# A decoder layer on one NeuronCore: layernorm's last step moved to VectorE, scratch parts written once per batch, and cross-attention divided by its sums in PSUM

## The chip, the core and the metric

The kernel runs on one core of a Trainium2 chip. A core has a matrix engine (TensorE, "PE" in the profile; its weight loads are "PEld"), three engines for elementwise work (VectorE, "DVE"; ScalarE, "ACT"; GpSimd, "POOL"), and SyncE ("SP"), which here only issues DMAs. Matrix products land in PSUM (8 banks of 128 partitions x 512 float32 here); everything else works in SBUF. The metric is the device time of one execution in microseconds, lower is better; the time of a kernel is the median of its runs.

## The reference

32 batches of 128 tokens with 128 features go through a post-norm decoder layer. Cut to what matters:

```python
x = layernorm(x + self_attention(x))          # 16 heads of 8; q = k = x, values x, then @ weight
x = layernorm(x + cross_attention(x, ctx))    # 16 heads of 8, scores masked to |i - j| <= 64
x = layernorm(x + two_layers(x))              # each: local attention (8 heads of 64), gated feed-forward

def layernorm(x):
    return (x - mean(x)) / sqrt(var(x) + 1e-5)

# cross-attention, per batch and head
scores = Q @ K.T / sqrt(8), masked
out    = softmax(scores) @ V                  # = (exp(scores - max) @ V) / sum(exp(scores - max))
y      = concat(out) @ Wo.T + bo
```

Each of the two layers has one more layernorm (with gain and bias) ahead of its feed-forward. So a batch meets five layernorms: after self-attention, after cross-attention, one in each layer, one at the end; 160 in all.

## The kernel before, in words

The 32 batches are cut into 10 groups of 1 to 4 (`SIZES`). Each group passes four stages: self-attention, cross-attention, layer 0, layer 1. A stage is a Python generator that records operations (`op(engine, ns, function, reads, writes, ...)`, L84) and yields after each batch; a due time `STARTS[g] / G + k * LAG * CLOSE[g]` with a spread per batch (end of the kernel) sorts the pieces of all stages into one list, so that several groups in different stages are interleaved.

`Plan.issue` (L132) then makes the real order by hand of a planner: every operation has a declared cost in ns, every buffer belongs to a ring (`Ring`, `Val`) of a few tiles, and the planner takes, engine by engine, the operation that can start first by these costs, looking at most `AHEAD` operations past the first one not yet placed and preferring the older one among those within `NEAR` ns. An operation that needs a buffer waits until the ring has one; `hold` reserves a buffer early; `KEEP` sets how many of a ring are left for older values; `port=True` keeps GpSimd and VectorE operations on SBUF from overlapping in the plan. The result is a fixed instruction order per engine; semaphores between engines do the rest. Rings: `m` (the 8 PSUM banks), `big` (23 wide tiles), `mid` (17), `xb` (6), `xc` (4), `sm` (24 small ones), `slots` (12 scratch areas in HBM).

What the change and the prediction touch:

- `layernorm` (L377): statistics on VectorE (L382, L389), the reciprocal root and the bias by four small GpSimd instructions (L397 to L400), and the last step x * r + q, one ScalarE instruction of 128x128 per batch (L407).
- `in_slots` (L494): queries and keys are split into three bfloat16 parts (ScalarE L500, L506; GpSimd L502, L508). Nine DMAs per group and tile write the three parts into nine slots of a scratch area in HBM, each DMA one part into one slot for all batches of the group (L518). `stacked` (L525) reads one batch back with the nine slots on 72 partitions (L528); it waits for all nine writes. Scores (`scores_of`, L540) are products over those 72 rows.
- `cross_batch` (L701): per half of the heads: scores with a mask, row maxima on VectorE (L421), exponentials on ScalarE (L466), transposes (L481) and copies (L488), then the product with the values (L722), whose output holds 32 rows of values and 32 rows of sums, in two column halves of the PSUM tile: `o.t[64 * c : 64 * c + 64, 0:P]`. ScalarE copies this to SBUF (L731). After both halves two transposes (L738) turn it, and VectorE takes a reciprocal of 16 sums per token (L748) and multiplies (L749).
- `cross_attention` (L634): after the batches of a group, `turned` (L362) transposes the result again (L373, one transpose per batch) and copies it (ScalarE, L367), for the projection (L687).
- ScalarE's copies of local attention's products are at L799 and L855, its exponentials at L466; VectorE's work of local attention is at L808, L831, L835, L838, L883 and L884, its residual add at L917; GpSimd's at L811, L812 and L822. Self-attention's products are at L577 and L606, its reciprocals and multiplies at L615 and L616; the projections of the layers at L794, L910, L942 and L962.

Of the kernel before, what the change touches and what calls it, by code (L numbers as in the profile page):

```python
# [11 lines left out]
AF = mybir.ActivationFunctionType  # L12
ALU = mybir.AluOpType
# [14 lines left out]

AHEAD = 290
LAG = 1.35  # L30
RINGS = (23, 17, 6, 4)
KEEP = (2, 4, 6)
NEAR = 60
EARLY = (0.1, 0.2)
CLOSE = (0.9, 0.85, 0.9, 1, 1, 1, 1.15, 1.0, 0.85, 0.95)
SPREAD = (1.3, 1.0, 0.7, 1.5)
LH, LD = 8, 64
# [194 lines left out]
def decoder_kernel(ctx: ExitStack, tc: tile.TileContext, a: dict, out: bass.AP):  # L232
    nc = tc.nc
# [5 lines left out]
    def ring(name, n, keep, shape, dtype=F32, pool=const):  # L239
        return Ring([pool.tile(shape, dtype, name=f"{name}{i}") for i in range(n)], keep)  # L240
# [7 lines left out]
    small = ring("sm", 24, 4, [P, 32])  # L248
# [3 lines left out]
    w_self, w_cross = Val(nothing), Val(nothing)  # L252
    w_layer = [Val(nothing) for _ in range(DEPTH)]
    mtring = ring("mt", 4, 1, [P, P], BF16)

# [3 lines left out]
    def group(v):  # L259
        return v[:, 0:512].rearrange("p (g d) -> p g d", g=G)  # L260
# [116 lines left out]
    def layernorm(src, dst, n):  # L377
# [26 lines left out]
        def apply():  # L404
            x, y = group(src.t), group(dst.t)
            for j in range(n):
                nc.scalar.activation(  # L407
                    y[:, j, :], x[:, j, :], AF.Identity,
                    scale=mv.t[:, 8 + j : 9 + j], bias=mv.t[:, 12 + j : 13 + j],
                )  # L410

        op("ACT", 425 * n, apply, [mv] + ([src] if src is not dst else []), [dst])

# [80 lines left out]
    def in_slots(src, n, keep_src, moving):  # L494
# [17 lines left out]
        for m in moving:  # L512
            t = Val(slots)
            for a in range(3):
                for b in range(3):
                    k = 3 * b + a if m else 3 * a + b
                    op("SP", P * 256 * n / 150,
                       lambda t=t, a=a, k=k: nc.sync.dma_start(  # L518
                           t.t[0:n, k].rearrange("j f t -> f j t"),
                           pv.t[:, a, every].rearrange("p (j t) -> p j t", j=n)),  # L520
                       [(pv, a)], [(t, k)])
            out.append(t)
        return out

    def stacked(t, j):  # L525
        v = Val(big, lambda t: t.bitcast(BF16)[0:72, 0:2048])
        op("SP", 72 * 4096 / 250,
           lambda: nc.sync.dma_start(  # L528
               v.t, t.t[j].rearrange("s (d h) t -> (s d) (h t)", d=8)), [t], [v])
        return v  # L530
# [103 lines left out]
    def cross_attention(g):  # L634
# [24 lines left out]
        def values():  # L659
# [14 lines left out]
           [w_cross], [x1], port=True)  # L674
        on = Val(mid)
        yield
        qs, = in_slots(qT, n, False, (False,))
        ks, = in_slots(kT, n, False, (True,))
        for j in range(n):
            cross_batch(j, stacked(qs, j), stacked(ks, j), vT, on)  # L680
            yield
        onT = turned(on, n)
        yp = Val(mring)

        def project():
            for j in range(n):
                nc.tensor.matmul(  # L687
                    yp.t[:, 128 * j : 128 * j + 128], group(onT.t)[:, j, :], woT,
                    start=True, stop=True,
                )  # L690

        op("PE", n * 228, project, [onT, w_cross], [yp])
        op("DVE", 160 + 135 * n,
# [6 lines left out]

    def cross_batch(j, qs, ks, vT, on):  # L701
        vb = Val(vbring)
# [4 lines left out]
           [vT], [vb])  # L707
        oS = Val(mid)
        for hh in range(2):
# [6 lines left out]

            o = Val(mring)

            def pe(o=o, et=et, hh=hh, vb=vb):
                for b in range(4):  # L720
# [7 lines left out]

            op("PE", 875, pe, [et, vb], [o], hold=[oS], tiling=("columns", "columns"))
            op("ACT", 260,  # L730
               lambda o=o, hh=hh: nc.scalar.copy(  # L731
                   oS.t[:, 128 * hh : 128 * hh + 128], o.t[:, 0:P]),
               [o], [(oS, hh)])
        ot = Val(mring)

        def back(ot=ot, oS=oS):
            for r in range(2):
                nc.tensor.transpose(  # L738
                    ot.t[:, 128 * r : 128 * r + 128], oS.t[:, 128 * r : 128 * r + 128], ident
                )  # L740

        op("PE", 260, back, [oS], [ot])
        rl = Val(small)

        def normal(ot=ot, rl=rl, j=j):
            v = ot.t[:, 0:256].rearrange("p (c s b d) -> p c s b d", c=4, s=2, d=8)
            r = rl.t[:, 0:16].rearrange("p (c b) -> p c b", b=4)
            nc.vector.reciprocal(r, v[:, :, 1, :, 0])  # L748
            nc.vector.tensor_tensor(  # L749
                group(on.t)[:, j, :].rearrange("p (c b d) -> p c b d", b=4, d=8),  # L750
                v[:, :, 0], r.unsqueeze(3).to_broadcast([P, 4, 4, 8]), ALU.mult,
            )

        op("DVE", 560, normal, [ot], [rl, (on, j)])


# [364 lines left out]
```

## Time and profile before

| | us |
|---|---|
| time, median of 3 runs (lowest to highest) | 1290.97 (1290.47 to 1292.42) |
| the profiled execution's own time | 1291.86 |
| its span from first to last instruction | 1290.10 |
| TensorE busy / VectorE busy | 1213.7 / 1003.5 |
| ScalarE busy / GpSimd busy | 1018.7 / 827.3 |
| DMA: bytes moved, mean rate | 91.43 MB, 71 GB/s |

The profile records one execution. Its parts: busy time of each engine; the span in 40 slices of 32 us, one digit per slice (9 is 90% or more); the chain of work that ended last, followed back from the last instruction, with its shares by engine; and groups of instructions, one line each: source line, engine, operation, output and input tiles, shapes and count, then busy time in us, the mean duration in ns, and the idle time of the engine just before these instructions with what ended it. Busy times of overlapping matmuls are not counted twice, so a group's busy time can be less than count times mean. DMAs show in the queue of the engine that issued them (SPq).

### The profile page before, as it was taken

The page shows a single profiled execution, that of the slowest core. Times are in us where ns is not written, and L with a number is a line of the kernel's source. Part 1 is how long each engine was busy: PE and PEld are TensorE (multiplying, and loading weights), DVE is VectorE, ACT ScalarE, POOL GpSimd, SP SyncE. Part 2 cuts the span into 40 slices and gives each one's busy share as a digit, 9 for nine tenths or more (in the row PEclk, how much of TensorE's full clock was granted, in tenths as well). Part 3 has the DMA queues.
Part 4 walks back from the last instruction along what each step waited for, and adds up shares of the span by engine and source line. Part 5 has one row for each costly group of instructions (what it writes and reads, how often), then busy time and mean ns, then how long its engine had stood idle before and what let it go on. Part 6 is the DMA issues. An engine that isn't in the chain of part 4 may idle for free.

```text
span 1290.1 us, 27567 instructions
## 1 busy us (share of the span) xinstructions
PE 1213.7 (94%) x9687; PEld 887.6 (69%) x9730; DVE 1003.5 (78%) x1974; ACT 1018.7 (79%) x2920; POOL 827.3 (64%) x1094
## 2 busy tenths in 40 slices
PE   7899999999999999989999999999999999999886
PEld 3777767767676776767677787667666776567654
DVE  2678788768986888777787887777899877888774
ACT  4467677878797779867888888778898897999874
POOL 1775676755867675854687476654876647975353
PEclk9899999999999999999999999999999999999988
DMA  8768443242415150434105141422300010000000
GB/s 219 215 158 226 119 101 82 54 121 52 95 32 148 29 119 7 92 83 120 51 2 131 30 120 32 99 60 61 84 3 10 4 35 1 9 2 1 2 9 17
DMA packets 173546, 91.43 MB, mean 71 GB/s; under 512 B 155488, under 2 KB 161504, under 8 KB 173152
## 3 DMA queue, kind: packets, MB, share of 16 engines
q1 hardware_dynamic: 173408, 89.67, 27.7%
q8 instruction: 77, 1.26, 0.4%
q14 instruction: 61, 0.50, 0.1%
HBM read 49.79 MB, written 39.85 MB: 69 GB/s over the span
## 4 chain that ended last, share of the span: by engine, by line
PE 60%; POOL 12%; ACT 11%; DVE 10%; issue 3%; DMA 2%; SPq 1%; POOLq 0%; ACTq 0%; DVEq 0%
PE m L794 8%; PE m L481 7%; PE m L606 6%; PE m L577 5%; PE m L942 5%; ACT big L466 4%; PE m L869 4%; PE m L910 4%; POOL sm L811 4%; PE m L898 3%; PE m L849 3%; PE m L540 3%; PE m L962 3%; PE m L722 3%; POOL big L626 3%
## 5 line engine op out<-in xcount | busy, mean ns | idle before, releaser
L466 ACT ACTIVATE big<-m,sm 128x128 f32<-128x128 f32 x1024 | 322.6, 399 | 49.9 <-DVE sm L421 41.8
L421 DVE TENSOR_REDUCE sm<-m 128x4 f32<-128x512 f32 x384 | 244.8, 680 | 79.0 <-PE m L540 38.6
L626 POOL TENSOR_TENSOR big<-big 128x512 f32<-128x512 f32 (+2 forms) x192 | 164.1, 854 | 90.0 <-DVE big L616 36.0
L811 POOL TENSOR_TENSOR sm<-sm,nhalf 128x16 f32<-128x16 f32 x64 | 202.2, 3160 | 29.4 <-DVE sm L808 28.0
L822 POOL TENSOR_TENSOR big<-big,layer_w 128x512 f32<-128x512 f32 x128 | 160.1, 1251 | 71.3 <-ACT big L799 65.9
L794 PE MATMUL m<-layer_w,mid 128*128 128x512 f32 x384 | 191.9, 605 | 4.8 <-ACT big L466 2.7
L481 PE MATMUL m<-ident,big 128*128 128x128 f32 x1024 | 147.5, 278 | 14.7 <-DVE big L884 5.5
L481 PEld LDWEIGHTS m<-ident,big 128*128 128x128 f32 x1024 | 116.9, 142 | 60.7 <-issue 23.1
L577 PE MATMUL m<-self_w,mid 128*128 128x512 f32 x256 | 129.8, 616 | 6.6 <-DMA self_w<-in_self_w 5.9
L606 PE MATMUL m<-big,big 128*128 128x129 f32 x1024 | 130.1, 279 | 1.3 <-DVE big L616 0.6
L606 PEld LDWEIGHTS m<-big,big 128*128 128x128 f32 x1024 | 122.9, 193 | 11.1 <-issue 5.2
L466 ACT ACTIVATION_READ_ACCUMULATOR big<-m,sm 128x1 f32 x512 | 118.1, 231 | 0.0
L616 DVE TENSOR_TENSOR big<-m,sm 128x384 f32<-128x384 f32 (+1 forms) x192 | 98.6, 514 | 6.8
L884 DVE TENSOR_TENSOR big<-big,sm 128x512 f32<-128x512 f32 x128 | 94.9, 741 | 4.8 <-DVE sm L883 0.4
L584 ACT COPY big<-m 128x512 f32<-128x512 f32 x128 | 74.1, 607 | 29.8 <-PE m L577 28.8
L838 DVE TENSOR_TENSOR big<-big,sm 128x1024 f32<-128x1024 f32 x64 | 87.5, 1368 | 11.2 <-POOL sm L812 9.3
L942 PE MATMUL m<-mid,layer_w 128*128 128x512 f32 (+7 forms) x240 | 91.9, 528 | 3.9 <-ACT mid L948 2.1
L540 PEld LDWEIGHTS <-big 72*128 72x128 bf16 x1024 | 71.6, 97 | 33.6 <-issue 14.9
L831 DVE TENSOR_TENSOR big<-big,layer_w 128x1024 f32<-128x1024 f32 x64 | 83.7, 1307 | 12.1 <-ACT big L799 12.0
L488 DVE COPY big<-m 128x512 f32<-128x512 f32 x128 | 83.2, 682 | 11.8 <-PE m L481 11.2
L855 ACT COPY big<-m 128x512 f32<-128x512 f32 x128 | 71.9, 604 | 25.3 <-PE m L849 23.5
L794 PEld LDWEIGHTS m<-layer_w,mid 128*128 128x128 f32 x384 | 63.1, 191 | 40.2 <-issue 23.6
(116 smaller groups left out, 2580.0 us busy)
## 6 DMA issues: line engine op xcount, KB each, us to landing
big<-slots SPq DMA_DIRECT2D x128, 288.0 KB
slots<-big SPq DMA_DIRECT2D x180, 128.0 KB
slots<-big SPq DMA_DIRECT2D x108, 96.0 KB
layer_w<-in_layer_w SPq DMA_DIRECT2D x2, 1877.0 KB
slots<-big SPq DMA_DIRECT2D x36, 64.0 KB
mid<-in_xt SPq DMA_DIRECT2D x5, 256.0 KB
mid<-in_xg SPq DMA_DIRECT2D x5, 256.0 KB
mid<-in_ct SPq DMA_DIRECT2D x5, 256.0 KB
```

The lines of the kernel that those rows point to most:

```text
L421: lambda b=b: nc.vector.tensor_reduce(nm.t[:, 4 * b : 4 * b + 4], s[b].t, AX.X, ALU.max, negate=True),
L466: nc.scalar.activation(e.t[:, h, :], s[b].t[:, h - 4 * b, :], AF.Exp, bias=nm.t[:, h : h + 1], accum_out=sums.t[:, h : h + 1] if sums else ...
L481: nc.tensor.transpose(tp.t[:, 128 * c : 128 * c + 128], e.t[:, 4 * b + c, :], ident)
L540: nc.tensor.matmul(s[b].t[:, i, :], st[:, h, :], mv[:, h, :], start=not window and i == 0, stop=i == 3,)
L577: lambda zp=zp, h0=h0: nc.tensor.matmul(zp.t, group(xT.t)[:, j, :], attn_w[:, h0 : h0 + 4, :], start=True, stop=True),
L606: nc.tensor.matmul(oz.t[:, i, :], e.t[:, h0 + i, :], zs.t[:, h0 + i, :], start=True, stop=True,)
L616: nc.vector.tensor_tensor(zs.t[:, h0 : h0 + n, 0:D], oz.t[:, 0:n, 0:D], rl.t[:, 0:n].unsqueeze(2).to_broadcast([P, n, D]), ALU.mult,)
L626: lambda n=n: nc.gpsimd.tensor_tensor(z(0, n), z(0, n), z(n, n), ALU.add),
L794: lambda hp=hp, i=i: nc.tensor.matmul(hp.t, group(hT.t)[:, j, :], wqkv[l][:, INNER * i : INNER * (i + 1)], start=True, stop=True),
L811: nc.gpsimd.tensor_tensor(rn.t[:, 0:16], rn.t[:, 0:16], nhalf, ALU.pow)
L822: nc.gpsimd.tensor_tensor(r2.t[:, :, :, d0 : d0 + 32], q[:, :, :, d1 : d1 + 32], tabs[l][:, :, d0 : d0 + 32].unsqueeze(2).to_broadcast([P, ...
L942: lambda t=t, off=off, c0=c0, m=m: nc.tensor.matmul(t.t[:m, every], w1[l][:, off + c0 : off + c0 + m], hT.t[:, every], start=True, stop=True),
```

## The change

Three edits, and new constants for the planner. (1) Layernorm's last step becomes a VectorE `tensor_scalar` with two per-partition scalars instead of a ScalarE activation. (2) Each write into the scratch slots now takes one part of one batch and writes it into three slots at once (the source is repeated); a read waits only for its own batch's three writes. (3) Cross-attention's product stays in its layout: VectorE takes the reciprocal of the 32 rows of sums (each over 128 tokens) straight from PSUM and multiplies the 32 rows of values with it, four instructions per half of the heads; the ScalarE copies, both transposes and the later `turned` go. (4) `AHEAD`, the stages' due times (`LAGS` for `LAG`), the rings, `KEEP`, `NEAR`, `EARLY`, `CLOSE` and `SPREAD` have new values, and the declared DMA costs fall.

```diff
-AHEAD = 290
-LAG = 1.35
-RINGS = (23, 17, 6, 4)
-KEEP = (2, 4, 6)
-NEAR = 60
-EARLY = (0.1, 0.2)
-CLOSE = (0.9, 0.85, 0.9, 1, 1, 1, 1.15, 1.0, 0.85, 0.95)
-SPREAD = (1.3, 1.0, 0.7, 1.5)
+AHEAD = 410
+LAGS = (0, 1.35, 2.75, 4.1)
+RINGS = (23, 16, 6, 4)
+KEEP = (2, 3, 5)
+NEAR = 0
+EARLY = (0, 0)
+CLOSE = (0.9, 0.85, 0.9, 1, 1, 1, 1.2, 1.05, 0.85, 1.1)
+SPREAD = (1.4, 1.0, 0.7, 1.5)
...
+    sring = ring("sums", 3, 1, [P, P])
...
             for j in range(n):
-                nc.scalar.activation(
-                    y[:, j, :], x[:, j, :], AF.Identity,
-                    scale=mv.t[:, 8 + j : 9 + j], bias=mv.t[:, 12 + j : 13 + j],
+                nc.vector.tensor_scalar(
+                    y[:, j, :], x[:, j, :], mv.t[:, 8 + j : 9 + j], mv.t[:, 12 + j : 13 + j],
+                    ALU.mult, ALU.add,
                 )
-        op("ACT", 425 * n, apply, [mv] + ([src] if src is not dst else []), [dst])
+        op("DVE", 200 * n, apply, [mv] + ([src] if src is not dst else []), [dst])
...
-            for a in range(3):
-                for b in range(3):
-                    k = 3 * b + a if m else 3 * a + b
-                    op("SP", P * 256 * n / 150,
-                       lambda t=t, a=a, k=k: nc.sync.dma_start(
-                           t.t[0:n, k].rearrange("j f t -> f j t"),
-                           pv.t[:, a, every].rearrange("p (j t) -> p j t", j=n)),
-                       [(pv, a)], [(t, k)])
+            for j in range(n):
+                for a in range(3):
+                    k = slice(a, 9, 3) if m else slice(3 * a, 3 * a + 3)
+                    op("SP", 3 * P * 256 / 190,
+                       lambda t=t, a=a, k=k, j=j: nc.sync.dma_start(
+                           t.t[j, k].rearrange("s f t -> f s t"),
+                           pv.t[:, a, 128 * j : 128 * j + 128].unsqueeze(1)
+                           .to_broadcast([P, 3, P])),
+                       [(pv, a)], [(t, (j, a))])
...
-        op("SP", 72 * 4096 / 250,
+        op("SP", 72 * 4096 / 290,
            lambda: nc.sync.dma_start(
-               v.t, t.t[j].rearrange("s (d h) t -> (s d) (h t)", d=8)), [t], [v])
+               v.t, t.t[j].rearrange("s (d h) t -> (s d) (h t)", d=8)),
+           [(t, (j, a)) for a in range(3)], [v])
...
-        onT = turned(on, n)
...
-            op("PE", 875, pe, [et, vb], [o], hold=[oS], tiling=("columns", "columns"))
-            op("ACT", 260,
-               lambda o=o, hh=hh: nc.scalar.copy(
-                   oS.t[:, 128 * hh : 128 * hh + 128], o.t[:, 0:P]),
-               [o], [(oS, hh)])
...
-                nc.tensor.transpose(
-                    ot.t[:, 128 * r : 128 * r + 128], oS.t[:, 128 * r : 128 * r + 128], ident
-                )
...
-            nc.vector.reciprocal(r, v[:, :, 1, :, 0])
-            nc.vector.tensor_tensor(
-                group(on.t)[:, j, :].rearrange("p (c b d) -> p c b d", b=4, d=8),
-                v[:, :, 0], r.unsqueeze(3).to_broadcast([P, 4, 4, 8]), ALU.mult,
-            )
-        op("DVE", 560, normal, [ot], [rl, (on, j)])
+            op("PE", 875, pe, [et, vb], [o], hold=[oT, sums], tiling=("columns", "columns"))
+            def normal(o=o, sums=sums, hh=hh, j=j):
+                for c in range(2):
+                    nc.vector.reciprocal(
+                        sums.t[64 * c : 64 * c + 32, :], o.t[64 * c + 32 : 64 * c + 64, 0:P]
+                    )
+                for c in range(2):
+                    r, q = 32 * (2 * hh + c), slice(64 * c, 64 * c + 32)
+                    nc.vector.tensor_tensor(
+                        group(oT.t)[r : r + 32, j, :], o.t[q, 0:P], sums.t[q, :], ALU.mult
+                    )
+            op("DVE", 980, normal, [o], [sums, (oT, (j, hh))])
...
-            at = STARTS[g] / G + k * LAG * CLOSE[g]
+            at = STARTS[g] / G + LAGS[k] * CLOSE[g]
```

More of the change, by code (lines that the diff above doesn't have):

```diff
@@ L674, in cross_attention @@
            [w_cross], [x1], port=True)
-        on = Val(mid)
+        oT = Val(mid)
         yield
@@ L679, in cross_attention @@
         for j in range(n):
-            cross_batch(j, stacked(qs, j), stacked(ks, j), vT, on)
+            cross_batch(j, stacked(qs, j), stacked(ks, j), vT, oT)
             yield
-        onT = turned(on, n)
         yp = Val(mring)
@@ L687, in project @@
                 nc.tensor.matmul(
-                    yp.t[:, 128 * j : 128 * j + 128], group(onT.t)[:, j, :], woT,
+                    yp.t[:, 128 * j : 128 * j + 128], group(oT.t)[:, j, :], woT,
                     start=True, stop=True,
                 )
-        op("PE", n * 228, project, [onT, w_cross], [yp])
+        op("PE", n * 228, project, [oT, w_cross], [yp])
         op("DVE", 160 + 135 * n,
@@ L699, in cross_attention, with cross_batch @@
         x2s[g] = x2
-    def cross_batch(j, qs, ks, vT, on):
+    def cross_batch(j, qs, ks, vT, oT):
         vb = Val(vbring)
@@ L707, in cross_batch @@
            [vT], [vb])
-        oS = Val(mid)
         for hh in range(2):
@@ L715, in cross_batch @@
                 turned_half(e, et, b, "DVE", e)
-            o = Val(mring)
+            o, sums = Val(mring), Val(sring)
             def pe(o=o, et=et, hh=hh, vb=vb):
@@ L727, in pe @@
                         )
-            op("PE", 875, pe, [et, vb], [o], hold=[oS], tiling=("columns", "columns"))
-            op("ACT", 260,
-               lambda o=o, hh=hh: nc.scalar.copy(
-                   oS.t[:, 128 * hh : 128 * hh + 128], o.t[:, 0:P]),
-               [o], [(oS, hh)])
[L734 to L738, printed above, removed]
-                    ot.t[:, 128 * r : 128 * r + 128], oS.t[:, 128 * r : 128 * r + 128], ident
-                )
[L742 to L749, printed above, removed]
-                group(on.t)[:, j, :].rearrange("p (c b d) -> p c b d", b=4, d=8),
-                v[:, :, 0], r.unsqueeze(3).to_broadcast([P, 4, 4, 8]), ALU.mult,
-            )
-        op("DVE", 560, normal, [ot], [rl, (on, j)])
+            op("PE", 875, pe, [et, vb], [o], hold=[oT, sums], tiling=("columns", "columns"))
[10 more added lines that the diff above has]
+            op("DVE", 980, normal, [o], [sums, (oT, (j, hh))])
     def shifted(src, n):
```

## The prediction

> **What bounds the kernel now.** I read the page's first parts, then a table of four stretches, then the groups of instructions with each shape kept apart. From the page: busy time by engine, the slices of TensorE (PE) and VectorE (DVE), and the chain that ended last.
>
> ```profile
> PE 1213.7 (94%) x9687; PEld 887.6 (69%) x9730; DVE 1003.5 (78%) x1974; ACT 1018.7 (79%) x2920; POOL 827.3 (64%) x1094
> ...
> PE   7899999999999999989999999999999999999886
> ...
> DVE  2678788768986888777787887777899877888774
> ...
> PE 60%; POOL 12%; ACT 11%; DVE 10%; issue 3%; DMA 2%; SPq 1%; POOLq 0%; ACTq 0%; DVEq 0%
> ```
>
> TensorE is busy in nearly every slice and carries 60% of the chain. The other engines stand at 64 to 79%, so each has room, but not much. The stretches (busy us of each engine in turn) say where:
>
> ```profile
> core 0: us, PE busy (x) PEld busy (x) DVE busy (x) ACT busy (x) POOL busy (x), PEclk, DMA share, GB/s
> 0.00:80.00 80.00, 66.25 (x449) 47.59 (x450) 37.41 (x98) 38.79 (x81) 43.01 (x108) 0.94 0.77 207
> 80.00:1080.00 1000.00, 962.15 (x7943) 709.75 (x7977) 809.23 (x1594) 814.02 (x2363) 654.43 (x856) 1.00 0.30 74
> 1080.00:1240.00 160.00, 150.31 (x1087) 104.77 (x1092) 132.62 (x212) 139.23 (x401) 109.22 (x92) 0.99 0.01 3
> 1240.00:1290.10 50.10, 34.94 (x213) 25.52 (x212) 24.21 (x72) 26.67 (x75) 20.68 (x40) 0.81 0.06 17
> ```
>
> The start (80 us) and the tail (50 us) are bound by latency. Between them, 1160 us, TensorE is busy 1112.5 (95.9%) and VectorE 941.9 (81%): 218 us of room. Whether the change fits into that room decides the case. The groups (busy, mean ns, idle before):
>
> ```profile
> L738 PE MATMUL m<-ident,mid 128*128 128x128 f32 x64 | 13.0, 283 | 0.0
> L373 PE MATMUL m<-ident,mid 128*128 128x128 f32 x96 | 18.2, 284 | 5.8 <-ACT mid L407 4.5 <-ACT big L855 0.4 <-DVE mid L749 0.4
> L731 ACT COPY mid<-m 128x128 f32<-128x128 f32 x64 | 17.7, 288 | 12.5 <-PE m L722 11.7
> L407 ACT ACTIVATE mid<-mid,sm 128x128 f32<-128x128 f32 x64 | 26.8, 492 | 8.5 <-POOL sm L400 8.5
> L749 DVE TENSOR_TENSOR mid<-m,sm 128x128 f32<-128x128 f32 x32 | 9.3, 291 | 1.1
> L748 DVE RECIPROCAL sm<-m 128x16 f32<-128x16 f32 x32 | 8.0, 251 | 11.3 <-PE m L738 10.9 <-PE m L442 0.4
> L615 DVE RECIPROCAL sm<-m 128x3 f32<-128x3 f32 x128 | 22.2, 174 | 29.6 <-PE m L606 22.9 <-ACT big L855 3.2 <-ACT mid L407 2.4
> L615 DVE RECIPROCAL sm<-m 128x2 f32<-128x2 f32 x64 | 10.2, 159 | 1.1 <-PE m L606 1.1
> L382 DVE BATCH_NORM_STATS2 sm<-mid 128x6 f32<-128x128 f32 x96 | 21.6, 278 | 7.5 <-ACT mid L769 3.7 <-POOL mid L630 3.5 <-ACT big L598 0.3
> L933 DVE TENSOR_SCALAR mid<-m,cross_w 128x128 f32<-128x128 f32 x2 | 0.8, 409 | 2.0 <-PE m L373 2.0
> ```
>
> To be seen: a reciprocal of 2, 3 and 16 elements takes 159, 174 and 251 ns. It grows by 6 to 7 ns per element, while the multiply beside it does 128 elements in 291.
>
> **TensorE loses** 96 transposes: 64 at L738 (13.0 us busy) and the 32 of the result at L373 (a third of 18.2: 6.1), so 19.1. In the chain around 1068 us such a transpose takes 0.11, so 96 x 0.11 = 10.6 if each stood on the path. I take 10.6; ends 6.4 (60% of it, the chain's share) and 19.1. No matmul is added.
>
> **ScalarE loses** the four groups of L407 (26.8 + 13.8 + 13.5 + 13.4 = 67.5), L731 (17.7) and 10 of the 20 copies at L367 (5.1 of 10.2). The changed program's order has 38 activation table loads for 34: 4 x 1.28 = 5.1 back. So 1018.7 - 85.2 = 933.5. At 72% it is less often late; I credit nothing, for TensorE's waits on it in the middle are 1 to 3 us each by line.
>
> **VectorE gains.** (a) 160 layernorm steps, 128x128 from SBUF to SBUF. No such row exists. Lower end 0.16 (the cast of the identity at L282, one source, same size), upper 0.41 (L933, the same operation out of PSUM); four L382 in a row take 0.86, 0.215 each. I take 0.25, nearest to those: 160 x 0.25 = 40 (26 to 65). (b) 128 multiplies of 32x128 out of PSUM: L749, 0.29 each, 37. Fewer partitions save nothing: at L952 85 partitions take 739 ns for 743 with 128. (c) 128 reciprocals of 32x128. Lower end: as any 128 elements from PSUM, 0.29, together 37. Upper end: along its own rows, 251 + 112 x 5.9 = 0.91 (from 3 to 16) or 251 + 112 x 6.6 = 0.99 (from 2 to 16). The reciprocals are the nearest row in kind, so I take 0.95: 122 us. (d) Gone: L748 and L749, 17.3. Sum: 1003.5 + 40 + 37 + 122 - 17 = 1185; with the lower end of (c) 1100.
>
> [...]
>
> **What it collides with.** Per half batch, (c) and (b) hold VectorE for 2 x 0.95 + 2 x 0.29 = 2.5 us, where ScalarE held its queue for 0.28. In the changed order two such blocks often stand together (29 of 64), and maxima (old L421), the copies of turned halves (L488) and adds (L917) stand behind: ScalarE's exponentials wait for the first, TensorE for the others. The layernorm step now makes VectorE wait for GpSimd (L400); ScalarE waited there 16.4 us in all (0 to 16; I take 0, for other work stands between statistics and step). The step reads and writes SBUF without the plan's port mark. VectorE's SBUF rows L831, L835 and L838 show medians of 1.22 and means of 1.30 to 1.37, so sharing costs 7 to 11%; that lies inside my 0.25.
>
> [...]
>
> **The slots.** Bytes and 256-byte rows stay the same; 360 write issues become 384 at a median of 0.50, +12 us on SP's queue, hidden: SP waits 334 us for L500 alone. Gains are at the start. There the queue's first 20 writes took 12.37 us and the last two of the first group's four reads went out from 22.32; the first scores began at 26.55, 0.60 after the matmuls before them. Now 12 writes serve that group instead of 18, so the reads land before those matmuls end: 0.6. At 46.7 scores wait for the slots again and TensorE then idles 4.53: 0 to 4.5. I take 3 together. Later the transfers are hidden behind the plan's lead.
>
> **Tail.** The three last layernorms stand on the path; a step costs 0.41 to 0.49 on ScalarE, 0.25 here: 2 us.
>
> **Sum.** In the 1160 us between start and tail VectorE must do 941.9 + 181.4 less the steps outside (22 of 160, 5.5) = 1118, which is 96%. An engine fed by three others did not do that: in a table of 40 us stretches its best held 37.4 (94%), the next 36.0 to 36.7 (90 to 92%); TensorE reaches 95.9. At 94% the stretch lasts 1189, 29 more; TensorE's saving is then hidden. Less start and tail (5): +24. Profiled execution 1291.86 (span 1290.10 and 1.76 around it): 1316; the median of the runs is 0.89 lower: **1315**. At 96% it is 1291, at 92% (1215) 1341.
>
> **Rivals.** (1) *The reciprocal runs like a multiply.* VectorE has 1100, in the stretch 942 + 91 = 1033 (89%), and TensorE stays the bound: 1290.97 - 10.6 - 3 - 2 = 1275; with 19.1 off TensorE 1267, with late waits 1285. For it: the rows of 2 to 16 elements read strided PSUM, whose cost may not be the divide's; against it: L749 reads strided too, at 128 elements in 291. It decides from about 0.7 us per reciprocal down: at 94% the stretch holds 1160 x 0.94 = 1090; less the present 942, and less 54 for steps and multiplies net of (d), that leaves 94 us for 128. (2) *Long reciprocals, covered.* The order is replanned everywhere (lead 410 for 290, later second and third stages), so VectorE could reach 96% and the freed TensorE and ScalarE take the waits: 1283 to 1293. Against: VectorE idles 43 us in the start already. (3) *The order, not the edits, moves the time.* The plan counts half a batch's divide as 980 ns; if it is longer, everything after it is late against plan, and a slots part made earlier brings nothing since the reads are ordered elsewhere: 1300 to 1345 even if VectorE is not full.
>
> **Numbers.** Forecast 0.47, (1) 0.36, (2) 0.11, (3) 0.06. What this kernel's measurement can tell from no change is 0.2%, 2.6 us. Faster: nearly all of (1) and half of (2), 0.40. Same: 0.07, from (2) and the forecast's lower edge. Slower: 0.53. The forecast alone spans 1291 to 1341; the range reaches down to (1): 1266 to 1338, leaving out some 15%.
>
> **What would show it.** The reciprocal's row at 32x128: 0.9 us or more, or near 0.29. VectorE near 90% of the span and TensorE under 92%: right; VectorE 85% and TensorE 94%: rival 1. Layernorm's row at 0.25. First scores before 26 us. ScalarE near 934. I am wrong if the reciprocal's time does not go by its elements, or if VectorE can be kept over 95% busy.

## The result, and the profile after

The changed kernel takes 1424.95 us (median of 4 runs, 1422.38 to 1425.55), the kernel before 1291.70 beside it (4 runs): ratio 1.1028, 95% interval 1.1013 to 1.1043. The forecast was 1315, its range 1266 to 1338. The direction was right; the loss is 133 us where 24 were forecast. The profiled execution took 1425.55 us with a span of 1423.7.

From the page of the changed kernel: busy time by engine, the slices of TensorE and VectorE, the chain that ended last.

```profile
PE 1259.2 (88%) x9634; PEld 907.2 (64%) x9634; DVE 1211.5 (85%) x2326; ACT 954.1 (67%) x2690; POOL 833.0 (59%) x1094
...
PE   7989798897888979998899999898899899899895
...
DVE  2698989787888798978998799899998989999974
...
PE 21%; DVE 11%; POOL 3%; ACT 3%; issue 2%; POOLq 0%; DVEq 0%; ACTq 0%
```

Three things are to be seen. TensorE lost 96 transposes, yet its busy time rose from 1213.7 to 1259.2. VectorE rose by 208 us, and still it is busy only 85%: no engine is full any more. And the chain could be followed only part way (its shares add up to 40%), so it does not name the bound here. The four stretches, with the columns as in the prediction's table:

```profile
0.00:80.00 80.00, 69.25 (x474) 48.92 (x475) 40.78 (x104) 41.41 (x89) 45.59 (x115) 0.96 0.85 229
80.00:1080.00 1000.00, 887.81 (x6932) 641.89 (x6930) 872.64 (x1685) 657.91 (x1844) 587.11 (x786) 0.95 0.28 70
1080.00:1240.00 160.00, 142.31 (x1060) 102.25 (x1061) 147.44 (x252) 123.81 (x379) 105.69 (x92) 0.94 0.04 10
1240.00:1423.70 183.70, 159.79 (x1173) 114.14 (x1171) 150.69 (x288) 131.00 (x383) 94.64 (x103) 0.96 0.02 7
```

TensorE did 962 us of work per 1000 in the long stretch before and does 888 now, at a granted clock of 0.95 for 1.00. The loss is spread over the whole run and has no single place. The span grew by 133.6 us; for TensorE that is 19.1 us of transposes gone, 64.6 us by which the rest of its busy time grew (1259.2 - 1194.6), and 88.1 us more idle time (76.4 before, 164.5 after).

The new rows of VectorE, each shape by itself (busy us, mean ns, idle before), and then all layernorm steps by line (ns: least/median/most):

```profile
L734 DVE RECIPROCAL sums<-m 32x128 f32<-32x128 f32 x128 | 122.3, 955 | 11.4 <-PE m L723 7.5 <-ACT mid L894 0.2
L739 DVE TENSOR_TENSOR mid<-m,sums 32x128 f32<-32x128 f32 x128 | 36.4, 284 | 4.0
L408 DVE TENSOR_SCALAR mid<-mid,sm 128x128 f32<-128x128 f32 x64 | 33.0, 573 | 7.5 <-POOL sm L401 7.3
```

```profile
L408 DVE TENSOR_SCALAR mid<-mid,sm x64: 329/342/1281, 236.9 to 1412.7; 128x128 f32<-128x128 f32 x64
L408 DVE TENSOR_SCALAR xb<-mid,sm x32: 333/346/1329, 50.2 to 1015.7; 128x128 f32<-128x128 f32 x32
...
  POOL sm L401: 15.5, 16
```

The reciprocal costs what was forecast (0.955 us for 0.95), the multiply too (0.284 for 0.29). The layernorm step does not: 0.34 us at the median, up to 1.33, and all 160 take 78.0 us for the 40 forecast. Its waits for GpSimd come to 15.5 us, the upper end of what was bounded. The long steps stand beside GpSimd's wide instructions, here two rows of the timeline (start, duration, engine and row):

```profile
115.43 1.27 POOL L629 TENSOR_TENSOR big<-big 128x512 f32<-128x512 f32 x1 [2.77 <-DVE big L619]
115.46 1.33 DVE L408 TENSOR_SCALAR xc<-xb,sm 128x128 f32<-128x128 f32 x1
```

So it is nearly everywhere: 107 of the 160 steps take under 0.4 us, and 53 more than that. Of the 53 all but one run beside a GpSimd instruction that takes 128 to 512 elements per partition from SBUF to SBUF, and 51 end 79 to 89 ns after that instruction does. Beside GpSimd's narrow instruction of 128x16 (L800, 3.2 us each) 11 steps took 0.33 to 0.35 us.

TensorE's waits of the changed kernel (line waited for: us in total, times, longest):

```profile
PE m L374 <- DVE mid L408: 14.6, 16, 4.7
PE m L482 <- DVE big L873: 13.4, 17, 3.1
PE m L482 <- DVE sm L872: 12.6, 5, 5.6
PE m L443 <- DVE mid L739: 11.5, 8, 2.4
PE m L482 <- DVE mid L739: 10.7, 9, 3.0
```

Summed over all lines of that view, TensorE waited 119.7 us for VectorE and 18.8 for ScalarE; before, 19.2 and 30.7. VectorE took ScalarE's place as the engine that is late. How this happens in one place is seen in the timeline of the changed kernel (start, duration, engine and row; in brackets the idle time before and what ended it):

```profile
402.81 0.60 DVE L739 TENSOR_TENSOR mid<-m,sums 32x128 f32<-32x128 f32 x2
...
403.44 1.94 DVE L734 RECIPROCAL sums<-m 32x128 f32<-32x128 f32 x2
403.46 0.61 PE L543 MATMUL m<-big,big 72*128 72x128 bf16 x8
...
405.41 0.60 DVE L739 TENSOR_TENSOR mid<-m,sums 32x128 f32<-32x128 f32 x2
406.05 0.29 DVE L906 TENSOR_TENSOR xb<-m,xc 128x128 f32<-128x128 f32 x1
406.07 0.70 PE L543 MATMUL m<-big,big 72*128 72x128 bf16 x8 [2.00 <-DVE mid L739]
...
406.26 0.17 DVE L872 RECIPROCAL sm<-sm 128x4 f32<-128x4 f32 x1
...
407.29 1.08 PE L482 MATMUL m<-ident,big 128*128 128x128 f32 x4 [0.52 <-DVE sm L872]
```

One half's divide holds VectorE for 2.54 us (1.94 + 0.60), and the PSUM bank that it reads is not free until the end. Scores need a bank: TensorE stands for 2.00 us. Behind the divide stand an add and local attention's normalisation, which the transposes of L482 need: another 0.52. VectorE itself is busy here from end to end, but elsewhere it idles 212 us in all.

### The profile page after: what moved, and what is told of

Same layout as the page of the kernel before. It is cut to its first block, busy times and chain, and to the rows that moved or that the text cites. A ratio compares the mean times of both kernels' runs of the same rounds, so it can differ in the third digit from the quotient of the medians.

```text
span 1423.7 us, 27539 instructions
## 1 busy us (share of the span) xinstructions
PE 1259.2 (88%) x9634; PEld 907.2 (64%) x9634; DVE 1211.5 (85%) x2326; ACT 954.1 (67%) x2690; POOL 833.0 (59%) x1094
## 5 line engine op out<-in xcount | busy, mean ns | idle before, releaser
L467 ACT ACTIVATE big<-m,sm 128x128 f32<-128x128 f32 x1024 | 321.1, 396 | 103.4 <-DVE sm L422 93.4
L800 POOL TENSOR_TENSOR sm<-sm,nhalf 128x16 f32<-128x16 f32 x64 | 206.0, 3219 | 71.8 <-DVE sm L797 62.1
L783 PE MATMUL m<-layer_w,mid 128*128 128x512 f32 x384 | 195.9, 622 | 6.1 <-DVE mid L739 4.5
L482 PE MATMUL m<-ident,big 128*128 128x128 f32 x1024 | 153.4, 286 | 45.4 <-DVE big L873 13.4
L811 POOL TENSOR_TENSOR big<-big,layer_w 128x512 f32<-128x512 f32 x128 | 155.3, 1214 | 55.4 <-ACT big L788 42.6
L482 PEld LDWEIGHTS m<-ident,big 128*128 128x128 f32 x1024 | 119.9, 146 | 98.2 <-issue 41.3
L580 PE MATMUL m<-self_w,mid 128*128 128x512 f32 x256 | 134.7, 639 | 10.7 <-DMA self_w<-in_self_w 5.4
L734 DVE RECIPROCAL sums<-m 32x128 f32<-32x128 f32 x128 | 122.3, 955 | 11.4 <-PE m L723 7.5
L489 ACT COPY big<-m 128x512 f32<-128x512 f32 x128 | 74.8, 600 | 59.1 <-PE m L482 52.1
L543 PEld LDWEIGHTS <-big 72*128 72x128 bf16 x1024 | 75.0, 100 | 47.2 <-issue 31.8
L587 ACT COPY big<-m 128x512 f32<-128x512 f32 x128 | 75.0, 604 | 40.6 <-PE m L580 39.3
L844 ACT COPY big<-m 128x512 f32<-128x512 f32 x128 | 71.5, 606 | 41.9 <-PE m L838 38.5
L543 PE MATMUL m<-big,big 72*128 72x128 bf16 x1024 | 91.3, 223 | 8.2 <-DVE mid L739 3.7
```

The costliest lines, as they stand in the source:

```text
L467: nc.scalar.activation(e.t[:, h, :], s[b].t[:, h - 4 * b, :], AF.Exp, bias=nm.t[:, h : h + 1], accum_out=sums.t[:, h : h + 1] if sums else ...
L482: nc.tensor.transpose(tp.t[:, 128 * c : 128 * c + 128], e.t[:, 4 * b + c, :], ident)
L489: lambda: copy(et.t[:, 4 * b : 4 * b + 4, :], tp.t.rearrange("p (c k) -> p c k", c=4)),
L543: nc.tensor.matmul(s[b].t[:, i, :], st[:, h, :], mv[:, h, :], start=not window and i == 0, stop=i == 3,)
L734: nc.vector.reciprocal(sums.t[64 * c : 64 * c + 32, :], o.t[64 * c + 32 : 64 * c + 64, 0:P])
L783: lambda hp=hp, i=i: nc.tensor.matmul(hp.t, group(hT.t)[:, j, :], wqkv[l][:, INNER * i : INNER * (i + 1)], start=True, stop=True),
```

## The experiments

The experiments put three questions: which part costs the time, what a change of order alone costs, and why the reciprocals are not covered. Differences are against the kernel before on the same chip (medians of 1290.17 to 1293.24), or between kernels that are named.

**The parts, in the changed kernel's program.** Reciprocals replaced by copies of the same shape, so that the result is multiplied by the sums and not divided; the declared cost is unchanged, hence also every queue's order:

```diff
-                    nc.vector.reciprocal(
+                    nc.vector.tensor_copy(
```

> The changed kernel with the same order, each reciprocal replaced by a copy of the same 32x128 from PSUM (so the result is multiplied by the sums, not divided). Length theory (the 0.955 us reciprocals, two per half batch where the plan counts 980 ns for all four instructions, make TensorE wait): a copy takes about 0.26, VectorE loses 128 x 0.69 = 89 us and TensorE's waits on VectorE (120 us) fall to some 30; time 1275 to 1300, granted clock 0.98 or more. Rival (the new constants' order, or layernorm's steps and the slots, carry it): no more than the 89 us go, 1336 or more.

Measured: 1334.88 (ratio 1.0340, 1.0324 to 1.0356), 90 us under the changed kernel. From the page, then the row of the copies:

```profile
PE 1223.9 (92%) x9634; PEld 887.4 (67%) x9634; DVE 1127.4 (85%) x2326; ACT 951.9 (71%) x2690; POOL 838.7 (63%) x1094
```

```profile
L734 DVE COPY sums<-m 32x128 f32<-32x128 f32 x128 | 36.9, 289 | 10.1 <-PE m L723 6.2 <-ACT mid L894 0.2
```

VectorE lost 84.1 us of work, and the time fell by 90. The share is the same 85%: what VectorE is spared leaves the span whole. So what the reciprocals last beyond a copy is two thirds of the loss; and with short ones the kernel would still be 44 us slower than before.

The divide's declared cost set near its real one (2.54 us), so that the planner sees it:

```diff
-            op("DVE", 980, normal, [o], [sums, (oT, (j, hh))])
+            op("DVE", 2500, normal, [o], [sums, (oT, (j, hh))])
```

> The changed kernel with the divide's declared cost raised from 980 to 2500 ns, so that the planner orders with what the trace shows (2 x 0.955 + 2 x 0.284 = 2.48); nothing else. If the wrong price in the plan makes the stalls: 1310 to 1345, where VectorE's 1200 us of work alone would put it, its share above 90%. If it is the load and the long hold themselves, whatever the order: 1390 to 1430.

Measured: 1443.96 (1.1195, 1.1177 to 1.1214), 19 us slower than the changed kernel. The honest price did not help. The order differs, and orders alone differ by more than 19 us (below), so what the price by itself is worth stays open; it is not the main cause.

Cross-attention's end as in the kernel before, everything else of the change kept; and layernorm's step back on ScalarE, everything else kept (in both the planner makes a new order):

> The changed kernel with cross-attention's end as before (ScalarE copies, two transposes, division of 16 sums per token, a turn per group) and its sums ring gone; layernorm on VectorE, the slots per batch and the new constants stay. Length theory: 1275 to 1300. Rival (order by the constants, or layernorm's steps blocking with GpSimd): 1340 or more.

> The changed kernel with layernorm's last step back on ScalarE. Length theory: the 78 us of steps leave VectorE, which remains late: 1345 to 1400. Rival (the steps, 0.342 at the median but up to 1.33 us each beside GpSimd, are what holds the chain): 1300 or less.

Measured: 1344.55 (1.0419, 1.0396 to 1.0441) and 1441.05 (1.1168, 1.1151 to 1.1185). Without the new cross end 80 us come back; without the layernorm step the kernel is 16 us slower, not faster.

**One part alone on the kernel before, planned anew.** Layernorm's step; the slots; the cross end (with 16 `mid` tiles and the ring of sums); the new constants of the planner alone:

> The kernel before with one part of the change: layernorm's last step on VectorE, old constants. By its row in the changed kernel (0.49 us mean, 78 us in all) VectorE goes to 1080 and ScalarE to 950; that leaves room on both. If each part is harmless without the others' load: 1280 to 1300. If the steps block with GpSimd so that they cost by themselves: 1310 or more.

> The kernel before with one part: each write takes one part of one batch into three slots, reads wait for their own batch, declared DMA costs lower; old constants. If slots are hidden as forecast: 1283 to 1295. If the earlier reads take buffers of the wide ring and so hold other work back: 1305 or more.

> The kernel before with one part: cross-attention divided in PSUM, with the sums ring (and 16 mid buffers for 17); old constants. VectorE gains 122 + 36 - 17 = 141 us and stands at 1145. Undoing this part alone took 80 us off the changed kernel, so by that 1370; by my forecast's way of counting (941.9 + 141 = 1083 of work in the 1160 us, at 94%: 1152, so no longer a stretch) 1280 to 1300.

> The kernel before with the new constants of the planner alone (lead 410, near 0, later stages, one mid buffer less). With cross-attention undone 54 us remained above the kernel before. If the constants' order makes them whatever the parts are: 1330 to 1360. If the constants are harmless: 1280 to 1300, and the 54 us belong to layernorm's steps or the slots.

| one part, planned anew | us | ratio (95%) |
|---|---|---|
| layernorm's step | 1367.34 | 1.0580 (1.0557 to 1.0604) |
| slots | 1325.33 | 1.0259 (1.0238 to 1.0279) |
| cross end | 1464.08 | 1.1328 (1.1310 to 1.1345) |
| constants | 1335.68 | 1.0339 (1.0321 to 1.0358) |

The four losses add up to 319 us (74 + 32 + 171 + 42), the whole change costs 133. Either the parts help each other, or every one of these numbers holds something else too. The slots' 32 us point to the second: those DMAs are hidden, and TensorE's work is the same. What all four share is a new order.

**A new order and nothing else.** The planner's lead in the kernel before set from 290 to 300, then to 280; in the changed kernel from 410 to 400. No operation is added, removed or made longer:

```diff
-AHEAD = 290
+AHEAD = 300
```

> The kernel before with the plan's lead 300 instead of 290 and nothing else: the same instructions in another order (about three quarters of each queue's rows move). Order theory (the kernel before stands on an order that fits the chip unusually well, and any other plan loses that, whatever is edited): 1310 to 1350. Work theory (the edits' own instructions make the time): 1288 to 1296.

> The kernel before with the plan's lead 280 for 290, nothing else. If any replanning loses the fit of the order: 1315 to 1350, as lead 300 did (1338). If 300 was an accident: 1288 to 1300.

> The changed kernel with lead 400 for 410, nothing else. If the changed kernel's order is an ordinary one for its instructions, as its 1335 with short copies beside the other replanned versions (1325 to 1344) suggests: 1410 to 1440. If its constants fit it as those of before fit the kernel before: 1455 or more.

Measured: 1338.39 (1.0368, 1.0352 to 1.0384), 1314.14 (1.0186, 1.0172 to 1.0200), and for the changed kernel 1471.86 (1.1415, 1.1399 to 1.1432), 47 us above its 1425. Such an edit costs 24 to 48 us: both kernels stand on orders that fit better than the neighbours tried, two of the one and one of the other. So a single part that is planned anew cannot be read finer than some 50 us, and the table above shows two parts above that, the cross end with its 171 us for certain and layernorm's step (74) only just. As far as these three neighbours tell, before and after both have this bonus, and of like size, so that little of it is in their difference.

**The parts in the order of before.** To take the order out, the next kernels keep every queue's order as it was, but for what the part itself moves, adds or leaves out. The operations keep their declared costs and engines in the planner's eyes, and only the instructions inside them change. First layernorm's step (declared as ScalarE's, issued on VectorE), then the slots (the first of three writes issues the repeated ones, the other two issue nothing):

```diff
-                nc.scalar.activation(
-                    y[:, j, :], x[:, j, :], AF.Identity,
-                    scale=mv.t[:, 8 + j : 9 + j], bias=mv.t[:, 12 + j : 13 + j],
+                nc.vector.tensor_scalar(
+                    y[:, j, :], x[:, j, :], mv.t[:, 8 + j : 9 + j], mv.t[:, 12 + j : 13 + j],
+                    ALU.mult, ALU.add,
                 )
```

> Layernorm's last step on VectorE, but planned as before (declared as ScalarE's 425 ns), so that every queue keeps its order and the 50 groups of steps move from ScalarE's queue to the same place in VectorE's. Order theory: 1285 to 1305, for the replanned version's 74 us came from the new order. Work theory (steps block with GpSimd and sit in VectorE's way): 1340 to 1370, as in the replanned version.

> The kernel before with three slots per write and one batch per write, planned as before (the writes stand where the first of each three stood), so that all engines keep their order; only SP's queue differs. If the slots cost nothing by themselves, as forecast: 1285 to 1294, the 32 us of the replanned version being order. If the repeated source or the 384 issues cost: 1300 or more.

Measured: 1320.98 (1.0237, 1.0212 to 1.0262) and 1290.21 (1.0002, 0.9992 to 1.0011). The step costs 31 us, the slots nothing: the 32 us of the replanned slots were the order.

Then the cross end, and all three parts together. The divide stands where ScalarE's copy stood; both transposes and `turned`'s are gone, and a ScalarE copy from SBUF to SBUF stays in the place of `turned`'s copy, with a few smaller ones where the result's tile was not yet there:

```diff
-            op("ACT", 260,
-               lambda o=o, hh=hh: nc.scalar.copy(
-                   oS.t[:, 128 * hh : 128 * hh + 128], o.t[:, 0:P]),
-               [o], [(oS, hh)])
+            def divide(o=o, hh=hh):
+                sums = oS.t[:, 128 * hh : 128 * hh + 128]
...
+                    nc.vector.reciprocal(
+                        sums[64 * c : 64 * c + 32, :], o.t[64 * c + 32 : 64 * c + 64, 0:P])
...
+                    nc.vector.tensor_tensor(
+                        to[r : r + 32, :], o.t[q, 0:P], sums[q, :], ALU.mult)
+            op("ACT", 260, divide, [o], [(oS, hh)])
...
-        op("PE", 260, back, [oS], [ot])
+        op("PE", 260, lambda: None, [oS], [ot])
```

> Cross-attention divided in PSUM, planned as before: the four VectorE instructions stand where ScalarE's copy was issued, the 96 transposes and the old division are left out, all else keeps its order (the result of a batch not yet given a buffer, and the group's turn, stay as ScalarE copies from SBUF). Order theory: 1290 to 1335, VectorE at 1145. Work theory (a 2.5 us block where 0.28 stood holds all behind it): 1400 to 1465, as in the replanned version.

> All three edits with the order of before kept: steps on VectorE, three slots per write (issued where the first of each three stood), division in PSUM. Order theory: 1295 to 1345, 80 or more below the changed kernel. Work theory: 1400 or more.

Measured: 1456.51 (1.1284, 1.1266 to 1.1302) and 1486.72 (1.1517, 1.1497 to 1.1536). In one fixed order the parts do add up: 31 + 0 + 166 = 197 us for 196 together. The changed kernel, 1424.95, is 62 us below that. Not all of it need be its order and rings: the copies that stay belong to these two kernels only. From the page of the kernel with the cross end alone, and the row of the smaller copies, for which ScalarE stands 27.4 us (the cost of that in time is not known):

```profile
PE 1267.9 (87%) x9634; PEld 912.2 (63%) x9634; DVE 1150.3 (79%) x2166; ACT 1016.1 (70%) x2879; POOL 821.7 (56%) x1094
...
L756 ACT COPY mid<-mid 64x128 f32<-64x128 f32 x23 | 6.9, 301 | 27.4 <-DVE mid L743 27.4
```

VectorE has 147 us more work than before, and the time is 166 longer, while VectorE is at 79% (78% before) and no other engine above 87%. Room by the page is plentiful, and none of it is used. Two explanations are left: the new data flow (what waits for the divide), or the mere time on VectorE's queue. The last three kernels tell them apart.

**The reciprocals' time by itself.** In the changed kernel, in its own order, one reciprocal over all 128 partitions of the product replaces the two over 32 (it also inverts the value rows, which nobody uses):

```diff
-                for c in range(2):
-                    nc.vector.reciprocal(
-                        sums.t[64 * c : 64 * c + 32, :], o.t[64 * c + 32 : 64 * c + 64, 0:P]
-                    )
+                nc.vector.reciprocal(sums.t, o.t[:, 0:P])
...
-                        group(oT.t)[r : r + 32, j, :], o.t[q, 0:P], sums.t[q, :], ALU.mult
+                        group(oT.t)[r : r + 32, j, :], o.t[q, 0:P], sums.t[64 * c + 32 : 64 * c + 64, :], ALU.mult
```

> The changed kernel, same order, with one reciprocal per half batch over all 128 partitions of the PSUM tile (its time goes by the 128 elements per partition) instead of two over 32; the two multiplies read the sums 32 partitions further. VectorE loses 64 x 0.955 = 61 us. If the reciprocals' time passes one to one into the total: 1360 to 1372. If VectorE's load counts only above a point already reached with the short copies (1335): 1335 to 1345. If the order carries the loss: 1410 or more.

Measured: 1354.33 (1.0504, 1.0488 to 1.0521), 71 us under the changed kernel. Its row by shape:

```profile
L733 DVE RECIPROCAL sums<-m 128x128 f32<-128x128 f32 x64 | 61.1, 955 | 8.6 <-PE m L723 7.3 <-ACT mid L891 0.2
```

A reciprocal of 128 partitions lasts as long as one of 32, 955 ns: VectorE has 62 us less to do (1149.6), and the span falls by 70. Half of the reciprocals' time in the change was avoidable.

Then the kernel before with 128 reciprocals that nobody needs, 32x128 on a dead SBUF tile, none of them waited for by anybody. Once in blocks of four behind each old division, once singly behind each VectorE copy of turned halves; the rest of every queue is as before:

```diff
+            for _ in range(4):
+                nc.vector.reciprocal(bvr[0:32, :], bvr[0:32, :])
```

```diff
+            if eng == "DVE":
+                nc.vector.reciprocal(bvr[0:32, :], bvr[0:32, :])
```

> The kernel before, order of all queues kept, with four reciprocals of 32x128 (3.8 us) on a tile that nobody reads any more, put behind each of the 32 old divisions: 122 us more on VectorE, which goes from 1003 to 1126. Room theory (my forecast's: VectorE's idle time takes it): 1291 to 1315. Pass-through theory (VectorE's idle time is waiting for other engines, and what stands behind a block in its queue is late by it): 1380 to 1430.

> The kernel before, order kept, with the same 128 reciprocals singly, one behind each of the 128 VectorE copies of turned halves: again 122 us. Room theory: 1291 to 1315. Pass-through of any added time: 1380 to 1430. If it is the length of the block that hurts and short pieces find gaps: 1315 to 1360.

Measured: 1414.23 in blocks (1.0948, 1.0930 to 1.0966), 1352.74 singly (1.0471, 1.0456 to 1.0487). The busy lines and the rows, blocks first:

```profile
PE 1255.5 (89%) x9687; PEld 912.5 (65%) x9730; DVE 1113.3 (79%) x2102; ACT 1021.9 (73%) x2920; POOL 829.7 (59%) x1094
...
L754 DVE RECIPROCAL bvr<-bvr 32x128 f32<-32x128 f32 x128 | 120.1, 938 | 3.3
```

```profile
PE 1233.0 (91%) x9687; PEld 891.7 (66%) x9730; DVE 1097.4 (81%) x2102; ACT 1021.0 (76%) x2920; POOL 833.2 (62%) x1094
...
L490 DVE RECIPROCAL bvr<-bvr 32x128 f32<-32x128 f32 x128 | 118.7, 927 | 0.0
```

120 us of useless work in blocks cost 122 us, though VectorE had 287 us of idle time before and none of its results are used. Spread out, the same work costs 60. (VectorE's busy time rises by 110 and 94 us and not by the rows' 120 and 119, for in the records neighbours overlap at their ends, and some other rows got shorter.) So the mere time on the queue is enough. How much of it shows differs (122 and 60 us); the two kernels differ in how the work is bunched and in where it stands in the queue, and no run here takes these apart. In the timeline of the kernel with the blocks:

```profile
99.70 3.85 DVE L754 RECIPROCAL bvr<-bvr 32x128 f32<-32x128 f32 x4
...
103.49 1.21 DVE L421 TENSOR_REDUCE sm<-m 128x4 f32<-128x512 f32 x2
...
104.62 1.26 DVE L488 COPY big<-m 128x512 f32<-128x512 f32 x2
104.76 0.19 POOL L435 CAST pad<-sm 128x8 bf16<-128x8 f32 x1 [2.71 <-DVE sm L421]
...
105.34 0.38 PE L540 MATMUL m<-big,big 72*128 72x128 bf16 x4 [2.41 <-DVE big L488]
```

The row maxima and the copies of turned halves stand behind the block. GpSimd waits 2.71 us for the first, TensorE 2.41 us for the second, and nobody waits for the block itself. The granted clock of TensorE is 1.00 in the first stretch of 3.41 us below and 0.50 in the second (a stretch, its busy time on PE, PEld, DVE, ACT and POOL, the clock, DMA share and GB/s):

```profile
102.70:106.11 3.41, 1.00 (x14) 0.88 (x12) 3.41 (x6) 0.59 (x1) 1.27 (x3) 1.00 0.85 204
106.12:109.53 3.41, 3.41 (x21) 3.19 (x22) 2.94 (x8) 0.00 (x0) 0.72 (x5) 0.50 0.85 252
```

Over the run, in that kernel's waits:

```profile
ACT big L466 <- DVE sm L421: 78.3, 45, 5.2
```

Before, ScalarE waited 41.8 us there; in the changed kernel 93.4. No version beat the kernel before; the one with the slots alone in the old order equals it.

## Why the prediction missed

**What held.** The reciprocal goes by its elements, 0.955 us for 128, and it decides the case: rival (1) needed 0.7 or less. The slope of the rows with 2 to 16 elements was a good guide. The multiplies came as forecast (36.4 us for 37). So did the start: the first scores begin at 25.75 for 26.55, and TensorE is busy 69.25 us of the first 80 for 66.25, the 3 us named. The 4.53 us that the prediction put down to the scores were TensorE's wait for a mask from GpSimd (`pad`, L436) behind them, and the scores had waited 0.23; now these waits are 1.05 and 1.43. The slots alone in the old order start earlier too (first scores at 24.14), and their time is 0.02% above the kernel before (interval -0.08 to 0.11): what is gained there does not reach the end. In that kernel a read still waits for the writes of its whole group.

**The step that failed** is "At 94% the stretch lasts 1189", with its premise "each has room". The best 40 us of an engine were taken for what it can reach over 1160, and idle time was taken for room. VectorE reached 88%: between 80 us and the last 50.1 of the span it worked 1140.6 of 1293.6. In the stretch that is 105 us more than forecast. Of it, 24 come from the work (1140.6 - 1118 = 22.6, at 94%), and 80 from the share. With the 5 us that the forecast took off for start and tail, and that these windows of fixed length do not show, this makes 110, the whole miss (1425 - 1315).

**Why there was no room.** VectorE's idle time before was mostly waiting for TensorE and ScalarE (181.8 and 58.5 of 287 us in its waits), and the plan fixes the order of its queue. A long instruction ahead of a short one that somebody needs makes that one late: in the timeline above the block lasts 3.85 us, and GpSimd waits 2.71 and TensorE 2.41 for what stands behind it. That the engine that is late in turn makes VectorE idle again at the next place is an inference, not shown step by step; VectorE's idle time was 287 us before and 295 with the blocks. The dummy blocks cost this time with no new data flow at all: +122 us for 120 us of work, at 79%. In each fixed order VectorE's share stays nearly what it was (78, 79 and 79% for before, the cross end and the blocks; 85, 85 and 85% for the changed kernel, the copies and the single reciprocal), and the span follows its work. The layernorm step and the single dummies stand at 81%, all three parts in the old order at 82%. With all three parts in the old order VectorE's 211 us of more work cost 196. By that the 181.4 us that the prediction had added up would have cost most of 181, and not 24 (an estimate: single parts passed on from half of their work, 31 us of time for 64 with layernorm's step, to all of it and more, 166 for 147 with the cross end); the changed kernel stands 62 us lower. Whether another engine's added time would do the same was not tried.

**The layernorm step** was mis-sized: 78 us for 40. Its median of 0.34 lies inside the bounds (0.16 to 0.41); 160 of those are 55 us. The other 23 us are steps of up to 1.33 us, and the trace shows beside what: nearly every one ends some 80 ns behind a wide GpSimd instruction (51 of 53). With the step alone in the old order the median is 0.34 too and the longest step 1.37. The prediction put what sharing costs at 7 to 11%; here it is these 23 us on 55. Not every GpSimd instruction does it: the 11 steps beside L800 took 0.33 to 0.35. No run here takes GpSimd's work away, so what the waiting costs in time is not measured. In the old order the step costs 31 us; in the changed kernel its removal costs 16. The second lies within what an order does, so its sign there stays open.

**ScalarE and TensorE.** ScalarE has 954.1 us for 933.5. The rows were subtracted whole, but in the records they overlap their neighbours: taken out of the trace of before, L407 and L731 free 65.9 us (1018.7 to 952.8) and not the 85.2 that they add up to. That it would be late less often was right (TensorE's waits for it fell from 30.7 to 18.8) and worth nothing. "TensorE's saving is then hidden" was right too; what was not thought of is that its remaining work takes longer in the changed kernel (1259.2 us for 1194.6, at a mean granted clock of 0.953 for 0.985; more below). In the last 50.1 us VectorE works 30.15 us for 24.21 and TensorE 35.80 for 34.94; the tail's 2 us are not to be seen.

**The rivals.** (1) failed on its price, and its number was wrong as well: the kernel with short copies takes 1334.88, not 1275. (2) failed like the forecast, by the share. (3) was half right: an order alone moves these kernels by 24 to 48 us, but before and after both stand on good ones as far as was tried, so it explains little of the 133; and a plan with the true price gave 1443.96, so that the reciprocals run late against the plan is not the main cost.

**Still open:** why the changed kernel stands 62 us below the three parts in the old order, how much of the difference between blocks and single reciprocals is their place, and what the price in the plan is worth apart from the order it leads to.

## What to carry to other kernels

An engine at 78% in a hand-made order need not have 22% of room: here its idle time was waiting, and work put on its queue, whose order the plan fixes, passed into the time whole when it came in blocks of some 4 us (122 for 120 us) and by half when it came in single microseconds at other places (60 for 119). Before a part is costed alone, measure what a change of order alone does (24 to 48 us here), and then test the part with every queue's order kept: only so did three parts add up here (197 us for 196). For an operation whose time goes by elements per partition, as the reciprocal's does (955 ns for 128 elements on 32 partitions and on 128), put as many partitions into one instruction as there are: that one line gave back 71 of the 133 us.

## What the runs showed of the hardware

- The reciprocal's time goes by the elements of a partition and not by the number of partitions: 955 ns for 32x128 and for 128x128 out of PSUM, 927 and 938 for 32x128 out of SBUF; 128x16 out of PSUM took 251. A copy of 32x128 out of PSUM takes 289.
- TensorE's mean granted clock was lower in kernels where it idled longer, though not in step with it: 0.985 at 76 us of idle time (before), 0.983 at 117 (the single dummies), 0.956 at 153 (the blocks), 0.953 at 165 (the changed kernel), 0.934 at 206 (all three parts in the old order). The matmuls of the same 9730 weight loads are busy 1213.7 us before, at a mean granted clock of 0.985, and 1255.5 with the dummy blocks, at 0.956. 3% of 1213.7 is 37 of these 42 us; the other 77 us by which that span grew (118.5) are idle time. With the same dummies singly the clock stays at 0.983, and the busy time still grows by 19.3 us, so the clock is not all of it. All kernels above 1400 us stand at 0.934 to 0.957. In the two stretches of the kernel with the blocks it was 1.00 while TensorE was busy 1.00 of 3.41 us, with a longest wait of 2.41, and 0.50 in the 3.41 us behind, all of them busy. What sets the clock is not shown.
- A VectorE step from SBUF to SBUF (0.34 us at 128x128) beside a GpSimd instruction over 128 to 512 elements per partition, also from SBUF to SBUF, ended some 80 ns behind that instruction (51 of the 53 long steps), up to 1.33 us after its own start; inside one over 16 elements (11 steps) it kept its 0.34. In the kernel before, the 192 instructions of L831, L835 and L838 (128x1024, median 1.22) took 1.30 to 2.30 us 37 times, each time beside a GpSimd instruction over 128 to 512 elements; inside one over 16 (44 times) they took 1.21 to 1.26.
- Writing one source into three slots by one DMA with the source repeated, for three separate DMAs, changes nothing measurable where the writes are hidden as here: 1290.21 and 1290.17 us (12 and 17 runs).
